# Order of the loads at the start, and the place of the condition gather, in a two-layer kernel with routed experts

## Chip, cores and metric

One core of a Trainium2 chip runs the whole kernel. The metric is device time in microseconds (us) of one execution; the time before is the median of three runs. TensorE is called PE, VectorE DVE, ScalarE ACT, GpSimd POOL and SyncE SP, as in the profile. SP and ACT only issue the plain DMAs here (ACT also computes); POOL issues the indirect ones, whose rows are picked by a list of indices.

## The reference, cut to what matters

The input x has 128 samples of 32 tokens of 256 numbers, 4096 tokens in all, and two index lists with one entry a sample.

```python
# layer 0
H  = x @ W.T                                  # per token
xa = x @ A[idx0].T                            # idx0: one of 8 adapters a sample, rank 16
h  = H + (xa @ Bm[idx0].T) * scalings[idx0]
scores = sigmoid(h @ gate_w.T)                # 8 experts
top, sel = top_k(scores, 2)
routed = sum over k of w2[sel_k] @ (silu(w1[sel_k] @ (h*top_k)) * (w3[sel_k] @ (h*top_k)))
shared = (silu(h @ ws1.T) * (h @ ws3.T)) @ ws2.T
x = x + shared + routed
# layer 1
c = einsum('bct,bcd->bdt', x, weights[idx1])  # a 32x32 mix of the tokens, one of 200 a sample
u = relu(quant(hadamard(c)) @ ternary(w_up).T) ** 2
x = x + quant(hadamard(u)) @ ternary(w_down).T
```

The "adapters' second factors" are Bm (tile bn, and BT in another layout), the "mixes" are `weights[idx1]` (tile wc).

## The kernel before

The 4096 tokens are 32 tiles of 128, in 8 groups of 4 tiles (NG = 8, GT = 4). The work has four stages.

**Loads and set-up (lines 140 to 209).** SP issues the big loads in the order in which they stand in the code, ACT the small ones: GW (gate), i1 (the mixes' indices), i0 (the adapters' indices, repeated on all partitions), sb (scalings). SP's order is wn, AT, xT[0], WT, bn, cst, BT, xT[1] to xT[7], ws, wall in two halves, ud. Each DMA uses one of eight semaphores in turn, so the ninth waits until the first has landed, and so on. cst is one tile of 962 columns with all constants; its first 640 are the identity, the Hadamard matrices and a scaled copy, the rest (from C_TRI on) small tables. Line 162, on POOL, gathers one 32x32 mix a sample (4 KB each, 512 KB) into wc; SP then writes wc to memory (cs, line 168) and reads it back as blocks on a diagonal (bd, four loads, line 181), which POOL has filled with zeros before (line 177). Lines 187 to 197 multiply the gate into W (from wn) and into Bm (from bn), all in one bank pt_gw; two copies on DVE put the result beside WT and BT, so that one matmul yields h and the gate's logits. Lines 203 to 209 make the adapters' mask and two copies of constants on DVE: upper, and idh (the identity in half precision, first used in layer 1).

**Projection and dispatch (lines 211 to 312).** `project(g)` makes pa (x by A, line 214), xa on DVE (line 216, times the mask), then for each of 4 tiles ph = xT by WT (line 226) plus xa by BT (line 229), which ACT copies into hc (line 230). `route(g)` computes scores, ranks and, through the matmuls pp (lines 282 and 283, which count the tokens ahead), the row of each of a token's two copies in an expert-sorted buffer xs in memory: row (285), pick (293), df and dest (298, 299). POOL then issues 8 indirect DMAs (line 303), each of which scatters 128 rows of hc to xs. The loop runs `project(g)` and then `route(g-1)`, so routing is one group behind.

**Slot table, shared expert, experts (lines 314 to 591).** SP reloads x in another layout into the buffers of xT (line 417, x[g] needs project(g) done). route(7), then the slot table (which expert has which of 72 tiles), the padding of xs, and the ternary weights (on DVE, lines 317 to 344). The shared expert runs for groups 0 to 5 (pt_h 429, pgs 439, hids 446, pos 454), then the experts over 36 pairs of tiles: SP fetches xin from xs (line 496) when all scatters have landed, PE transposes and multiplies (504, 530, 547, 556), POOL scatters the results to yt (line 563). Last come the shared expert's groups 6 and 7.

**Layer 1 (lines 594 to 777).** 16 pairs of tiles in a pipeline of 8 steps: combine on POOL (608), the mix by bd (616), Hadamard, quantize, up, relu squared, the outer Hadamard steps on POOL and DVE (694 to 697), quantize, down.

The order of instructions on each engine is made by a scheduler from the program's order and its dependences. The last stage's POOL order is the program's own.

Of the kernel before, what the change touches and what calls it, by code (L numbers as in the profile page):

```python
# [17 lines left out]
B, T = 128, 32  # L18
# [20 lines left out]
C_ID, C_H, C_HS, C_TRI, C_E16, C_N16 = 0, 128, 256, 640, 704, 712  # L39
# [5 lines left out]
def tile_kernel(  # L45
# [20 lines left out]
    nc = tc.nc  # L66
# [14 lines left out]
    def evac(dst, src):  # L81
# [7 lines left out]
    cst = cpool.tile([P, NCONST], F32, name="cst")  # L89
    ident = cst[:, C_ID : C_ID + P]  # L90
# [5 lines left out]
    xT = [  # L96
        cpool.tile([P, 2, GT * P], F32, tag="x", name=f"xT{g}", bufs=NG) for g in range(NG)
    ]
    bd = cpool.tile([P, NT, P], F32, name="bd")
# [4 lines left out]
    idh = cpool.tile([P, P], F16, name="idh")  # L104
# [5 lines left out]
    cs = dram.tile([B, T * T], F32, name="cs")  # L110

    with tc.tile_pool(name="moe", bufs=1) as moe, tc.tile_pool(name="work1", bufs=2) as work1:
# [12 lines left out]
        with tc.tile_pool(name="stage", bufs=1) as stage:  # L125
            wn = stage.tile([P, 2, D], F32, name="wn")
            bn = stage.tile([P, 2, P], F32, name="bn")
            i0 = stage.tile([P, B], I32, name="i0")
            i1 = stage.tile([B, 1], I32, name="i1")
            sb = stage.tile([P, E], F32, name="sb")  # L130
            wc = stage.tile([B, T * T], F32, name="wc")
# [3 lines left out]
            AT = stage.tile([P, 2, P], F32, name="AT")  # L135
# [3 lines left out]

            nc.scalar.dma_start(GW, gate)  # L140
            nc.sync.dma_start(wn, W.rearrange("(c p) d -> p c d", p=P))
            nc.scalar.dma_start(i1, idx1.rearrange("(b o) -> b o", o=1))
            nc.sync.dma_start(AT, AT_)
            nc.sync.dma_start(xT[0], xT_[0])
            nc.scalar.dma_start(
                i0, idx0.rearrange("(o b) -> o b", o=1).partition_broadcast(P)
            )
            nc.scalar.dma_start(
                sb, scal.rearrange("(o e) -> o e", o=1).partition_broadcast(P)
            )  # L150
            nc.sync.dma_start(WT[:, :, :D], WT_)
            nc.sync.dma_start(bn, Bm)
            nc.sync.dma_start(cst, consts)
            nc.sync.dma_start(BT[:, :D], BT_)
            for g in range(1, NG):
                nc.sync.dma_start(xT[g], xT_[g])
            nc.sync.dma_start(ws, shared_)
            nc.sync.dma_start(wall[:, : E * WCOL // 2], experts[:, : E * WCOL // 2])
            nc.sync.dma_start(wall[:, E * WCOL // 2 :], experts[:, E * WCOL // 2 :])
            nc.sync.dma_start(ud, updown)  # L160

            nc.gpsimd.indirect_dma_start(
                out=wc,
                out_offset=None,
                in_=cw.rearrange("s c d -> s (c d)"),
                in_offset=bass.IndirectOffsetOnAxis(ap=i1, axis=0),
            )
            nc.sync.dma_start(cs, wc)

            zeros = stage.tile([P, ROW], F32, name="zeros")  # L170
            cnt = stage.tile([P, E], F32, name="cnt")
# [3 lines left out]
            nc.gpsimd.memset(ones, 1.0)  # L175
            nc.gpsimd.memset(half, HALF)
            nc.gpsimd.memset(bd, 0.0)
            csv = cs.rearrange("(n q) (c d) -> q c n d", q=4, d=T)
            for q in range(4):
                s = slice(32 * q, 32 * q + 32)  # L180
                nc.sync.dma_start(bd[s, :, s], csv[q])


            pt = bank("t", "pt_gw")
# [21 lines left out]
                mask, i0, cst[:, C_N16 : C_N16 + 1], scol, ALU.is_equal, ALU.mult  # L206
            )
            nc.vector.tensor_copy(upper, cst[:, C_U : C_U + P])
            nc.vector.tensor_copy(idh, ident)

            def project(g):
                pa = bank("x", f"pa{g}")
# [181 lines left out]
            def pad():  # L394
# [10 lines left out]
                for e in range(E):  # L405
                    ins = nc.sync.dma_start(xs[bass.ds(rows[e], P), :], zeros).ins
                    tc.declare_no_dep(ins, group="xs", reason="no pair has a row of the padding")
                    tc.add_to_no_dep_group("xs", ins)

            xg = []  # L410
            for g in range(NG):
                project(g)
                if g > 0:
                    route(g - 1)
            for g in range(NG):
                xg.append(cpool.tile([P, GT, D], F32, tag="x", name=f"x{g}", bufs=NG))
                nc.sync.dma_start(xg[g], xt[g])
            route(NG - 1)
            slot_table()
            pad()  # L420
            ternary_weights()
# [50 lines left out]
        with tc.tile_pool(name="work2", bufs=3, reuse_waits="tile") as work:  # L472
# [105 lines left out]
            a, b, c_, tos = {}, {}, {}, {}  # L578
# [281 lines left out]
```

## Time and profile before

| | |
|---|---|
| three timed runs | 452.76, 451.7, 452.3 us; median 452.3 |
| profiled execution | 447.77 us |
| its span, first to last instruction | 446.0 us, mean granted PE clock 0.943 |
| PE / DVE / ACT / POOL busy | 370.8 / 263.1 / 164.4 / 226.5 us |
| projection starts (first ph) | 13.43 us from the span's start |
| first scatter / end of the last | 28.19 / 126.48 us |
| shared expert's first matmul (pgs) | 102.38 us |
| experts' first transpose (pt_s) | 151.59 us |
| layer 1's first combine on POOL | 291.10 us |

How to read it: times in a view run from the span's start. A line of the timeline gives start, length, engine, source line, operation, out<-in with the tiles' names, shape and count, and in brackets how long the engine was idle before and what ended that ("remote" is a semaphore's step that the profile can put down to no instruction; "issue" is a start that no recorded wait explains). The page shows the span also as 40 slices of 11.15 us, each digit a busy share in tenths.

### The profile page before, as it was taken

The numbers are of one execution on the slowest core, as the hardware profiler recorded it, in microseconds if no ns is written. First come the engines' busy times: TensorE is split into PE (matmuls) and PEld (weight loads), VectorE is DVE, ScalarE is ACT, GpSimd is POOL, SyncE is SP. The second block draws the span as 40 slices with busy tenths as digits, with TensorE's granted clock in tenths as the row PEclk, the third lists the DMA queues.
The fourth block names the chain that finished last, engine by engine and source line by source line (L and its number), as shares of the span: only waits on it lengthen the run. The fifth ranks groups of instructions, "written<-read, shape, count | busy, mean of one in ns | idle before, by whom it ended". The sixth has DMA issues, their size and how long they took to land.

```text
span 446.0 us, 6493 instructions
## 1 busy us (share of the span) xinstructions
PE 370.8 (83%) x2055; PEld 289.6 (65%) x2055; DVE 263.1 (59%) x711; ACT 164.4 (37%) x328; POOL 226.5 (51%) x227
## 2 busy tenths in 40 slices
PE   3999292847399899999899899988888878899864
PEld 2676171633166588887787778566777767789753
DVE  0366351527744556555465454345899899988872
ACT  1120110103021144444344243326365664576752
POOL 4037475765820025554655555589656664533340
PEclk9999698797599999999999999999699999999998
DMA  6999343423442134544444412266122220111012
GB/s 225 418 413 294 113 148 134 142 107 128 170 142 61 49 100 152 170 152 139 136 152 146 155 62 75 72 221 208 49 84 104 73 72 25 37 36 49 24 49 71
DMA packets 38881, 57.49 MB, mean 129 GB/s; under 512 B 9277, under 2 KB 28735, under 8 KB 38464
## 3 DMA queue, kind: packets, MB, share of 16 engines
q1 hardware_dynamic: 31600, 39.17, 26.9%
q0 software_dynamic: 6672, 17.84, 10.9%
q8 instruction: 17, 0.28, 0.2%
q10 hardware_dynamic: 576, 0.08, 0.1%
q14 instruction: 16, 0.13, 0.1%
HBM read 33.93 MB, written 24.18 MB: 130 GB/s over the span
## 4 chain that ended last, share of the span: by engine, by line
PE 54%; DVE 21%; POOL 9%; another core or an unknown queue 6%; issue 4%; ACT 4%; DMA 2%; SPq 0%; DVEq 0%; ACTq 0%; POOLq 0%
PE pg L530 15%; PE po L556 7%; PE pgs L439 7%; PE ph L226 5%; POOL x L608 4%; PE ph L229 4%; DVE b L696 4%; PE pr L709 3%; PE pt_s L504 3%; DVE b L697 3%; PE pos L454 3%; POOL a L695 3%; POOL a L694 2%; PE pa L214 2%
## 5 line engine op out<-in xcount | busy, mean ns | idle before, releaser
L563 POOL DMA_INDIRECT yt<-y,to x72 | 70.3, 976 | 89.3 <-DVE cm L513 39.0
L303 POOL DMA_INDIRECT xs<-hc,dest x64 | 65.6, 1024 | 54.7 <-issue 22.2
L530 PE MATMUL pg<-wall,xTs 128*128 x288 | 76.8, 390 | 4.4 <-DVE cm L513 2.2
L530 PEld LDWEIGHTS pg<-wall,xTs 128*128 128x128 f32 x288 | 49.2, 190 | 16.5 <-DVE hid L539 5.5
L539 DVE SCALAR_TENSOR_TENSOR hid<-pg,c,sil 128x128 f32<-128x128 f32 x72 | 25.1, 348 | 47.3 <-ACT sil L538 39.0
L709 PE MATMUL pr<-cst,b 128*128 128x128 f32 x256 | 39.8, 301 | 12.4 <-DVE b L696 10.7
L538 ACT ACTIVATE sil<-pg,c 128x128 f32<-128x128 f32 x72 | 26.5, 368 | 61.8 <-PE pg L530 55.1
L608 POOL TENSOR_TENSOR x<-x,y 128x512 f32<-128x512 f32 x32 | 43.3, 1360 | 6.3 <-PE pgs L439 5.0
L709 PEld LDWEIGHTS pr<-cst,b 128*128 128x128 f32 x256 | 34.5, 207 | 16.1 <-issue 8.1
L230 ACT COPY hc<-ph 128x264 f32<-128x264 f32 x32 | 12.0, 380 | 80.5 <-PE ph L229 34.4
L556 PE MATMUL po<-wall,hidT 128*128 x144 | 37.7, 381 | 0.0
L229 PE MATMUL ph<-BT,xa 128*128 128x264 f32 x64 | 22.4, 438 | 18.4 <-DVE xa L216 18.4
L226 PE MATMUL ph<-WT,xT 128*128 128x264 f32 x128 | 36.3, 411 | 0.3 <-DVE WT L196 0.3
L722 POOL TENSOR_TENSOR dq<-m,kq 128x2 f32<-128x2 f32 x16 | 3.1, 197 | 59.8 <-DVE m L716 59.8
L632 PE MATMUL pf<-cst,yT 128*128 128x256 f32 x128 | 32.4, 391 | 1.4 <-ACT yT L624 1.4
L439 PE MATMUL pgs<-hT,ws 128*128 128x512 f32 x64 | 31.7, 641 | 0.0
L226 PEld LDWEIGHTS ph<-WT,xT 128*128 128x128 f32 x128 | 26.1, 205 | 8.3 <-issue 2.9
L725 ACT ACTIVATE q<-pr,half,sc 128x512 f16<-128x512 f32 x32 | 23.2, 774 | 18.0 <-DVE sc L721 18.0
L696 DVE TENSOR_TENSOR b<-a 128x512 f32<-128x512 f32 x16 | 20.5, 1282 | 13.7 <-POOL a L695 13.7
L229 PEld LDWEIGHTS ph<-BT,xa 128*128 128x128 f32 x64 | 13.0, 213 | 22.7 <-DVE xa L216 19.8
L285 DVE TENSOR_TENSOR row<-pp,cst 128x32 f32<-128x32 f32 x8 | 1.5, 192 | 42.6 <-remote 30.3
L648 ACT ACTIVATE q<-pf,half,sc 128x256 f16<-128x256 f32 x32 | 16.4, 562 | 27.3 <-DVE sc L644 27.2
(132 smaller groups left out, 720.8 us busy)
## 6 DMA issues: line engine op xcount, KB each, us to landing
xin<-xs SPq DMA_DIRECT2D x72, 136.0 KB
y<-yt SPq DMA_DIRECT2D x16, 512.0 KB
xT<-in_xT SPq DMA_DIRECT2D x8, 512.0 KB
x<-in_x SPq DMA_DIRECT2D x8, 512.0 KB
out<-o SPq DMA_DIRECT2D x16, 256.0 KB
wall<-in_experts SPq DMA_DIRECT2D x2, 1536.0 KB
yt<-y,to POOLq DMA_INDIRECT x72
xs<-zeros SPq DMA_DIRECT2D x8, 136.0 KB
```

What stands on the lines that cost most here:

```text
L226: nc.tensor.matmul(ph, xT[g][:, k, cols], WT[:, k], start=(k == 0), stop=False)
L229: nc.tensor.matmul(ph, xa[:, cols], BT, start=False, stop=True)
L303: ins = nc.gpsimd.indirect_dma_start(out=xs, out_offset=bass.IndirectOffsetOnAxis(ap=dest[:, i, n : n + 1], axis=0), in_=hc[g][:, n], in_o ...
L439: nc.tensor.matmul(pg, ws13[:, k, i], hT[:, k], start=(k == 0), stop=(k == 1))
L530: nc.tensor.matmul(pg[:, i].rearrange("p a f -> p (a f)"), xT[:, i, k], wall[:, bass.ds(w + k * D, D)], start=(k == 0), stop=(k == 1),)
L538: nc.scalar.activation(sil[:, i], pg[:, i, 0], AF.Silu, scale=ci)
L556: nc.tensor.matmul(po[:, i], hT[:, i], wall[:, bass.ds(w + 2 * D, D)], start=True, stop=True)
L563: ins = nc.gpsimd.indirect_dma_start(out=yt, out_offset=bass.IndirectOffsetOnAxis(ap=to[:, i : i + 1], axis=0), in_=y[:, i], in_offset=Non ...
L608: nc.gpsimd.tensor_tensor(v, v, y2[:, :, r], ALU.add)
L632: nc.tensor.matmul(pf[:, i], yT[:, k, i * P : (i + 1) * P], had256[k], start=(k == 0), stop=(k == 1),)
L696: nc.vector.tensor_tensor(b[:, 0:2], a[:, 0:2], a[:, 2:4], ALU.add)
L709: nc.tensor.matmul(pr[:, f * P : (f + 1) * P], b[:, f, i * P : (i + 1) * P], had, start=True, stop=True,)
```

## The change

The instructions are the same but for one DMA more (cst is loaded in two parts). They are put in another order:

- SP now issues wn, **bn**, AT, xT[0], WT, **cst's last 322 columns**, BT, xT[1] to xT[4], **cst's first 640 columns**, xT[5] to xT[7], and the rest as before. bn stood behind WT, and cst in one piece behind bn.
- ACT issues GW, i0, sb and then i1; i1 stood second.
- The gather (POOL), cs and the four bd loads (SP) are in a function `mixes()`, called when project(2) and route(1) have been written. On POOL the gather stands, by an order held fixed, between the scatters of group 1 and those of group 2; before, it stood ahead of all scatters. On SP, cs now stands behind x[2], and the bd loads behind x[3]; before, cs stood ahead of x[0] and bd behind x[1].
- idh is copied behind route(7) (its place on DVE is held by the same means, between dest of group 7 and the slot table's st); before, it was copied ahead of the mask.
- On PE, bn's two products stand ahead of pa(0) instead of behind it, and in the first group the adapters' part of tile 0 (line 229) two products earlier. Otherwise PE's order is that of before.

```diff
             nc.scalar.dma_start(GW, gate)
             nc.sync.dma_start(wn, W.rearrange("(c p) d -> p c d", p=P))
-            nc.scalar.dma_start(i1, idx1.rearrange("(b o) -> b o", o=1))
-            nc.sync.dma_start(AT, AT_)
-            nc.sync.dma_start(xT[0], xT_[0])
             nc.scalar.dma_start(
                 i0, idx0.rearrange("(o b) -> o b", o=1).partition_broadcast(P)
             )
+            nc.sync.dma_start(bn, Bm)
             nc.scalar.dma_start(
                 sb, scal.rearrange("(o e) -> o e", o=1).partition_broadcast(P)
             )
+            nc.sync.dma_start(AT, AT_)
+            nc.sync.dma_start(xT[0], xT_[0])
+            nc.scalar.dma_start(i1, idx1.rearrange("(b o) -> b o", o=1))
             nc.sync.dma_start(WT[:, :, :D], WT_)
-            nc.sync.dma_start(bn, Bm)
-            nc.sync.dma_start(cst, consts)
+            nc.sync.dma_start(cst[:, C_TRI:], consts[:, C_TRI:])
             nc.sync.dma_start(BT[:, :D], BT_)
             for g in range(1, NG):
                 nc.sync.dma_start(xT[g], xT_[g])
+                if g == 4:
+                    nc.sync.dma_start(cst[:, :C_TRI], consts[:, :C_TRI])
...
-            nc.gpsimd.indirect_dma_start(
-                out=wc,
-                out_offset=None,
-                in_=cw.rearrange("s c d -> s (c d)"),
-                in_offset=bass.IndirectOffsetOnAxis(ap=i1, axis=0),
-            )
-            nc.sync.dma_start(cs, wc)
...
-            csv = cs.rearrange("(n q) (c d) -> q c n d", q=4, d=T)
-            for q in range(4):
-                s = slice(32 * q, 32 * q + 32)
-                nc.sync.dma_start(bd[s, :, s], csv[q])
...
             nc.vector.tensor_copy(upper, cst[:, C_U : C_U + P])
-            nc.vector.tensor_copy(idh, ident)
...
+            def mixes():
+
+                tc.keep_in_program_order(
+                    nc.gpsimd.indirect_dma_start(
+                        out=wc,
+                        out_offset=None,
+                        in_=cw.rearrange("s c d -> s (c d)"),
+                        in_offset=bass.IndirectOffsetOnAxis(ap=i1, axis=0),
+                    )
+                )
+                nc.sync.dma_start(cs, wc)
+                csv = cs.rearrange("(n q) (c d) -> q c n d", q=4, d=T)
+                for q in range(4):
+                    rows = slice(32 * q, 32 * q + 32)
+                    nc.sync.dma_start(bd[rows, :, rows], csv[q])
+
             xg = []
             for g in range(NG):
                 project(g)
                 if g > 0:
                     route(g - 1)
+                if g == 2:
+                    mixes()
...
             route(NG - 1)
+            tc.keep_in_program_order(nc.vector.tensor_copy(idh, ident))
             slot_table()
```

## The prediction

> **What bounds the kernel now.** I read the page's slices first, then the chain that ended last, then the waits of the stretch in which the chain leaves the program, then GpSimd's (POOL's) timeline there. The slices have PE at 8 or 9 tenths from slice 11 on, but at 7, 3, 9, 9, 8, 9, 9 and lower before, and the window sums say the same: 14.76 us busy of 14.76 between 13.43 and 28.19, but 16.70 of 25.56, 16.15 of 24.49 and 16.84 of 25.19 in the three stretches that follow. All that the change moves acts ahead of 119 us, so that is where it must be priced. The chain of waits, in order of time (start, length, what):
>
> ```profile
> 42.03 5.93 another core or an unknown queue
> ...
> 64.99 11.48 another core or an unknown queue
> ...
> 97.00 3.83 another core or an unknown queue
> 101.28 1.11 PE pt_h L429 x4
> ...
> 118.84 1.22 PE pos L454 x2
> ```
>
> Three times the chain stands in a wait that no instruction ends. After 118.84 it is TensorE, without a hole up to the experts (32.76 us busy of 32.76 up to 151.60). Who waits, between 28 and 104 us (total, times, longest):
>
> ```profile
> DVE row L285 <- remote: 30.3, 3, 11.5
> ACT hc L230 <- remote: 23.9, 6, 6.0
> ...
> PE ph L229 <- DVE xa L216: 18.4, 2, 9.5
> ```
>
> Both "remote" waits are for TensorE's counter alone: the matmuls before them are dispatched long before (the pp of group 2 at 40.77, its reader starts at 50.99). The trace's semaphore records show that counter nearly standing still and then making eight steps between 50.80 and 51.13, again five steps between 76.44 and 76.63, and again from 100.83. POOL's timeline lies beside these times:
>
> ```profile
> 28.19 0.98 POOL L303 DMA_INDIRECT xs<-hc,dest  x1 [22.02 <-DVE s L239]
> ...
> 47.39 0.96 POOL L303 DMA_INDIRECT xs<-hc,dest  x1 [0.30 <-issue]
> 53.75 1.11 POOL L303 DMA_INDIRECT xs<-hc,dest  x1 [5.39 <-issue]
> ...
> 73.17 0.96 POOL L303 DMA_INDIRECT xs<-hc,dest  x1 [0.30 <-issue]
> 78.24 1.02 POOL L303 DMA_INDIRECT xs<-hc,dest  x1 [4.12 <-ACT s L237]
> ...
> 97.55 0.96 POOL L303 DMA_INDIRECT xs<-hc,dest  x1 [0.30 <-issue]
> 103.43 1.13 POOL L303 DMA_INDIRECT xs<-hc,dest  x1 [4.92 <-ACT hT L86]
> ```
>
> The scatters run in bursts of 16, two groups of tokens each, 1.27 us apart (0.96 + 0.30). A burst ends at 48.35, 74.13 and 98.51; its last scatter lands at 49.66 and 75.42 (the third's last packet ends at 99.60); the counter comes free at 50.80, 76.44 and 100.83, so 2.45, 2.31 and 2.32 us after POOL's last issue. Then route needs 2.9, 1.8 and 2.6 us to hand POOL the next rows. The reading that I go by: **a burst of software DMAs holds back TensorE's increments until it has drained.** Why it does so the trace does not say; that the release follows the drain three times within 0.14 us is what I rely on. The period is then 16 scatters plus drain plus route, and the place of PE at 101.28 is set by POOL's first scatter and by what is in the bursts. From 101.28 to 118.84 VectorE (DVE) sets the time (13.84 us busy of 15.41): route(7), the slot table and the ternary weights stand ahead of hids.
>
> **The change part by part.** The profiled execution took 447.77 us, its span is 446.0, with 1.77 around it; the median of the three timed runs is 452.3, 4.5 above. I add differences only, and lay them on the median.
>
> 1. *bn and the small constants ahead of x.* The start now:
>
> ```profile
> 8.76 3.75 PE L214 MATMUL pa<-xT,AT 128*128 128x512 f32 x4 [2.87 <-DMA xT<-in_xT]
> ...
> 12.30 0.86 PE L187 MATMUL pt_gw<-GW,bn 128*128 128x8 f32 x4
> ...
> 13.20 0.17 DVE L196 COPY WT<-pt_gw 128x16 f32<-128x16 f32 x1 [11.78 <-PE pt_gw L187]
> ...
> 13.43 0.94 PE L226 MATMUL ph<-WT,xT 128*128 128x264 f32 x3 [0.27 <-DVE WT L196]
> ...
> 13.64 0.22 DVE L209 CAST idh<-cst 128x128 f16<-128x128 f32 x1
> ```
>
> The reader is to see that bn's matmuls stand behind pa in PE's order and that WT's copy, and with it ph, waits for them. In the new order they follow wn's matmuls (ending 5.89; AT, issued at the place that bn gets, lands at 4.53), in time in which PE is idle. pa ends at 12.51, so ph would start 13.43 - 12.51 = 0.92 sooner. Against it: xT[0] is issued one DMA later on SP (2.24 instead of 1.77), 0.47. I take -0.45, with 0 and -0.92 as ends. The mask and xa are ready well before PE needs them in both orders (xa at 14.84, used at 15.76), and from ph on PE has no hole up to the first scatter, so POOL starts 0.45 sooner, near 27.74.
>
> On the clock: pa's four matmuls take 3.75 here and 1.88 at 18.87, and full clock is recorded from 13.02. The Trainium skill ("TensorE: Matmul & The Clock Gate", Part 1) says that the clock is set by a free-running window of about 3.4 us of activity, not counted from the kernel's start; by it the new hole between bn's matmuls and pa could make the full clock come one window later, which at half speed would turn the gain into an estimated loss of up to 1.2 us. The sum is left at the row.
>
> 2. *i1 last on ACT, cst in two parts, its head behind xT[4].* One more SP issue (0.33 to 0.47 us) in a queue whose next waits are for landed loads. The head (identity, Hadamard) is first read at 93.48 by pt_h. Cost 0; without that cover, a late head would hold PE at pt_h.
>
> 3. *idh moved behind route(7).* At 13.64 it costs nothing (PE is dense); now it stands in DVE's full stretch before hids. Issue to issue it takes 0.14 (13.64 to 13.78), 0.22 at most: +0.14.
>
> 4. *The gather leaves the start.* It is POOL's L162 at 5.05, its data moves from 9.17 to 12.96, and it lands at 13.43, beside the x loads. xT[0] has landed by then (8.17) and later ones are far ahead of use (xT[7] is needed at 86), so removing it gives 0.
>
> 5. *The gather comes between the scatters of groups 1 and 2.* On POOL: 1.13 + 0.30 = 1.43 more in burst 1, behind which group 2's scatters stand. Taken alone this is hidden: POOL is idle for 5.39 us there. But by the reading above burst 1 is now 17 long, and the counter comes free after the gather has drained. Its packets: 8 of 4096 B an engine at 159 ns, 1.27 us, where a scatter has 2 of 4352 B at 190 ns, 0.38: +0.89. So the release moves by 1.43 + 0.89 = +2.32, and with it row, dest, burst 2, burst 3 and PE at 101.28. Ends: 0 (gathers into SBUF do not hold PE) and the gather's own row, issue to landing 13.43 - 5.05 = 8.38, where the same from a scatter is 75.42 - 73.17 = 2.25; that is 1.43 + 6.13 = +7.56. I stay near the low row: at 45 to 51 us the hardware queue moved no packet in the trace, while at 9 to 13 it moved 180 to 410 KB/us beside the gather.
> The Trainium skill ("DMA: Bandwidth & Descriptors", Anatomy of one DMA) gives a software DMA about 2.0 us fixed and the rest at 436 GB/s; by that an estimated 3.2 us for 512 KB, against the 8.38 of the row. By the rule the sum below stays, by the row it would be 5.2 higher.
>
> 6. *SP's queue.* cs now waits for the gather on SP, and x[3], the four bd loads and x[4..7] stand behind it. x[3] waits for PE's project(3) anyway (issued at 50.87 now), the four bd issues take 4.94 us and x[4] is not issued before 59 either; x[g] is first read in shared_down behind 124, bd from the last stage on, behind 281. Cost 0. The bd loads (4 x 1024 packets of 128 B) move from beside burst 1 to beside burst 2; POOL's pitch in burst 1 was 1.27 with them and 1.27 without in burst 2, so 0.
>
> 7. *After 126.* POOL's last scatter ends at 126.48 and PE takes up the experts at 151.59: some 20 us of slack, so POOL's own 1.43 costs nothing there.
>
> Sum: -0.45 + 0.14 + 2.32 = **+2.0 us**: 449.8 for a profiled run, 452.3 + 2.0 = 454.3 as a median.
>
> **The rivals.** (a) *The gather does not hold the counter*: only scatters, which write to memory, do. For it: no gather stands beside a PE at work in this trace. Against: nothing sets its queue apart from theirs. Then -0.45 + 0.14 = -0.3: 452.0, and 451.5 with the whole 0.92. (b) *Faster*: the first hold is not the burst's but that of bd's small packets; they start at 36 us, and PE's counter is first late by more than 2 us at 37.34, 9.1 us into the burst, against 10.3 and 11.8 us in the others. With them gone group 2's rows are there when the gather has been issued, and POOL goes on at 49.3 instead of 53.75: -4.2 - 0.3, so 447.8. It decides if group 2's pp is counted before POOL runs dry at 49.3. Against: bursts 2 and 3 are held as long without any such packet. (c) *Much slower*: the longer burst lets group 2's increments trickle through just before its end; POOL then adds 8 scatters to the same burst, nothing drains until 62, and the pairs become {0,1,2}, {3,4}, {5,6}: PE's release moves from 100.83 to about 112.5, +11.7: 464. (d) That the change does not do what it says: the order of the instructions shows it does; PE's, DVE's and ACT's streams are otherwise the same.
>
> **How the numbers follow.** What a measurement tells from no change is 0.2%, 0.9 us. Forecast 0.50 (its own range 452.9 to 456), (a) 0.22, (b) 0.18, (c) 0.10. Slower: 0.48 of the forecast (a release nearer 1.4 than 2.3 would fall within 0.2%) and (c), 0.58. Faster: (b), and 0.06 of (a) with a better start, 0.24. Within: 0.18. The range reaches down to (b) with room for a second gap, 446.5, and up to the gather's own row, 452.3 - 0.45 + 0.14 + 7.56 = 459.6; it leaves out (c) and the end of (b), under 0.2.
>
> **What would show it.** Right: ph starts near 13.0 and the first scatter near 27.7; the gather follows the 16th scatter; the counter's leap comes near 52.7, group 2's first scatter near 55.6, PE's pt_h near 103.2, all later stretches as long as now. Wrong: group 2's scatter straight behind the gather (b or c), a leap still near 50.4 (a), or a burst 2 or 3 of another length, which would mean that the order of the holds is not tied to the drain.

## The result, and the profile after

The changed kernel took 451.09 us (median of 20 runs, 449.39 to 452.81), the kernel before 451.29 us beside it (20 runs, 446.25 to 452.76). The ratio is 1.0004 with a 95% interval of 0.9983 to 1.0025: no change that can be measured, where +2.0 us was forecast. The profiled executions are 450.77 us after (span 449.0) and 447.77 before (span 446.0); those 3.0 us between two single executions lie within the kernel's own spread, and the one before is among its quicker ones. A run more than 1.5% above the fastest of its kernel on its chip counts as slow and is left out of a ratio: none here, but in set 1 below 10 of 29 runs of the kernel before, 5 of 12 of the loads alone and 8 of 12 of the gather alone.

The start after, TensorE (PE) in its timeline (start, length, engine, line, operation, operands, count; in brackets the idle time ahead of it and what ended it):

```profile
5.66 1.00 PE L177 MATMUL pt_gw<-GW,bn 128*128 128x8 f32 x4
8.39 3.75 PE L203 MATMUL pa<-xT,AT 128*128 128x512 f32 x4 [1.73 <-DMA xT<-in_xT]
11.94 1.68 PE L215 MATMUL ph<-WT,xT 128*128 128x264 f32 x6
```

bn's products now stand ahead of pa, in idle time, and nothing stands between pa and ph: ph starts 3.54 us behind pa's start (4.67 before). pa starts at 8.39 where it was 8.76, although xT[0] is issued at 2.23 instead of 1.77.

GpSimd (POOL) in the same view:

```profile
26.86 1.34 POOL L292 DMA_INDIRECT xs<-hc,dest  x1 [21.98 <-DVE s L228]
...
46.27 0.96 POOL L292 DMA_INDIRECT xs<-hc,dest  x1 [0.30 <-issue]
47.53 0.97 POOL L402 DMA_INDIRECT wc<-in_cond,i  x1 [0.30 <-issue]
53.92 1.12 POOL L292 DMA_INDIRECT xs<-hc,dest  x1 [5.42 <-issue]
```

The first scatter comes 1.33 us sooner (28.19 before), group 2's first 0.17 us later (53.75): the stretch between them grew from 25.56 to 27.06. The later two stretches are 0.28 and 0.37 us longer here (24.77 and 25.56); in the other two executions with a gather in the first burst (set 1 below) they are as before (24.57 and 25.10, 24.54 and 25.18; 24.49 and 25.19 before). PE's pt_h comes at 102.11 (101.28 before, 103.2 forecast) and its first pos at 120.72 (118.84). Of those last 1.88 us, 1.12 arise between row of group 6 and row of group 7 (7.66 for 6.54), where half clock was granted for 10.24 us in one piece and for 6.83 before; that this is the reason is not shown. What waits between 28 and 104 us, then the chain that ended last:

```profile
DVE row L274 <- remote: 33.2, 3, 11.8
ACT hc L219 <- remote: 30.8, 6, 11.4
...
PE ph L218 <- DVE xa L205: 20.7, 2, 10.9
```

```profile
41.01 7.38 another core or an unknown queue
48.80 2.48 another core or an unknown queue
...
65.14 11.78 another core or an unknown queue
...
87.13 11.39 another core or an unknown queue
...
102.11 1.12 PE pt_h L437 x4
```

The same three holes are there. So far the result looks as if 1.3 us of gain and 1.5 us of cost cancelled. The experiments show the cost on one kind of chip only.

### The profile page after: what moved, and what is told of

It reads as the page before. It is cut to its first block, busy times and chain, and to the rows that moved or that the text cites. A ratio compares the mean times of both kernels' runs of the same rounds, so it can differ in the third digit from the quotient of the medians.

```text
span 449.0 us, 6497 instructions
## 1 busy us (share of the span) xinstructions
PE 369.9 (82%) x2055; PEld 288.2 (64%) x2055; DVE 263.0 (59%) x711; ACT 164.4 (37%) x328; POOL 226.1 (50%) x227
## 4 chain that ended last, share of the span: by engine, by line
PE 48%; DVE 21%; POOL 9%; another core or an unknown queue 9%; issue 5%; ACT 3%; DMA 3%; SPq 1%; DVEq 0%; POOLq 0%; ACTq 0%
PE pg L538 13%; PE pgs L447 7%; PE po L564 6%; PE ph L215 5%; DVE b L704 4%; DVE b L705 3%; PE pr L717 3%; POOL x L616 3%; PE ph L218 3%; PE pos L462 3%; POOL a L703 3%; PE pt_s L512 3%; POOL a L702 3%; PE pa L203 2%
## 5 line engine op out<-in xcount | busy, mean ns | idle before, releaser
L538 PE MATMUL pg<-wall,xTs 128*128 x288 | 78.2, 396 | 7.0 <-DVE hid L547 3.6
L717 PE MATMUL pr<-cst,b 128*128 128x128 f32 x256 | 37.9, 291 | 13.7 <-DVE b L704 11.3
L717 PEld LDWEIGHTS pr<-cst,b 128*128 128x128 f32 x256 | 32.7, 197 | 17.5 <-issue 8.1
L447 PE MATMUL pgs<-hT,ws 128*128 128x512 f32 x64 | 33.0, 663 | 0.0
L733 ACT ACTIVATE q<-pr,half,sc 128x512 f16<-128x512 f32 x32 | 23.2, 774 | 16.9 <-DVE sc L729 16.9
L704 DVE TENSOR_TENSOR b<-a 128x512 f32<-128x512 f32 x16 | 20.5, 1282 | 13.7 <-POOL a L703 13.7
```

The costliest lines, as they stand in the source:

```text
L447: nc.tensor.matmul(pg, ws13[:, k, i], hT[:, k], start=(k == 0), stop=(k == 1))
L538: nc.tensor.matmul(pg[:, i].rearrange("p a f -> p (a f)"), xT[:, i, k], wall[:, bass.ds(w + k * D, D)], start=(k == 0), stop=(k == 1),)
L704: nc.vector.tensor_tensor(b[:, 0:2], a[:, 0:2], a[:, 2:4], ALU.add)
L717: nc.tensor.matmul(pr[:, f * P : (f + 1) * P], b[:, f, i * P : (i + 1) * P], had, start=True, stop=True,)
```

## The experiments

**Theory**: the loads' order gains between one and two microseconds at the start, and the gather costs about as much in the first burst, because software DMAs in a burst hold back the increments of TensorE's semaphore. **Rivals**: the gather holds nothing (rival a of the prediction); the start's gain is no gain of the loads but a matter of when the full clock is granted; or the hold is not a property of the burst.

Five sets were run, on five chips; the first of them behaves as the chip of the result does, and may be the same. Each set's ratios are against the kernel before on the same chip. Marks are of single profiled executions, in us: the *first stretch* runs from the first scatter to group 2's first, *row* is the start of that DVE instruction for a group, *PE's restart* the start of the first pos, behind the last hole, and the *scatters' end* the end of POOL's last scatter to xs.

### Set 1: the parts of the change, and a second gather

*The loads alone* (gather, cs and bd at the start as before; idh late):

```diff
             nc.sync.dma_start(ud, updown)
+            nc.gpsimd.indirect_dma_start(
...
+            nc.sync.dma_start(cs, wc)
...
-                if g == 2:
-                    mixes()
```

> The loads in the new order and the late copy of idh, with the gather, its store and the reloads where they stood before. Theory T (a burst of software DMAs holds TensorE's counter until it has drained): the earlier start passes through every burst, first scatter near 26.9 us as in the changed kernel, row of group 2 near 49.7 (50.99 before, 51.33 changed), row of group 6 near 99.8, and the time 1.2 us below before, ratio 0.997. Rival R (the first hold ends by something that stands fixed against the loads): row of group 2 stays near 51 and the ratio is 1.000.

Measured: 0.9961 (0.9915 to 1.0007); over all runs the median is 449.33, of the kernel before 448.66. Marks: first scatter 27.93, first stretch 25.61, row of group 2 at 50.79 and of group 6 at 100.86, all three marks with an expectation 1.0 to 1.1 us later than expected.

*The gather alone*, an edit of the kernel before (its loads and idh stay; the gather, cs and bd leave the start):

```diff
                     route(g - 1)
+                if g == 2:
+                    mixes()
```

> The loads and idh in the old order, only the gather, its store and the reloads amid the dispatch. Theory T: first scatter 28.2, the counter's release 1.7 us later because the burst is one DMA longer, row of group 2 near 52.7, row of group 6 near 102.7, time +1.7 us, ratio 1.004. Rival R: the gather costs nothing, row of group 2 near 51, ratio 1.000.

Measured: 0.9948 (0.9888 to 1.0009), a ratio that rests on 4 of the 12 runs; over all of them the median is 450.87, 2.2 above the kernel before, so the total says neither loss nor gain. Marks: first scatter 29.70, first stretch 26.58, so +1.0 by the mark; row of group 2 is 24.24 us behind the first scatter (22.80 in the kernel before).

*The whole change, with the gather behind all scatters*:

```diff
-                if g == 2:
-                    mixes()
...
             route(NG - 1)
+            mixes()
```

> The changed kernel with the gather behind the scatters of all groups. Theory T: no burst holds the gather, row of group 2 near 49.7, row of group 6 near 99.8, time 1.2 us below before, ratio 0.997. Rival: SP now issues the store and the reloads ahead of the experts' rows; if these come later than TensorE's end of the shared groups (151.6 before) the time is above before.

Measured: 1.0004 (0.9973 to 1.0035), median 448.17. Marks: first scatter 27.43, first stretch 25.52, row of group 2 at 50.38 and of group 6 at 100.16.

*The gather twice* (the second into a tile of its own; the output is the same):

```diff
                 tc.keep_in_program_order(
                     nc.gpsimd.indirect_dma_start(
                         out=wc,
...
+                tc.keep_in_program_order(
+                    nc.gpsimd.indirect_dma_start(
+                        out=wc2,
...
+                nc.sync.dma_start(cs2, wc2)
```

> The changed kernel with the gather done twice in the same place, into two tiles, and stored twice. Theory T: the first burst has 18 DMAs, so the release moves by the same 1.7 us again: row of group 2 near 53.0 (51.33 changed), later bursts unchanged in length, row of group 6 near 103.3. Rival R: row of group 2 stays at 51.3.

Measured: 448.01 us in one run; first scatter 26.91, first stretch 27.29. POOL's timeline in it:

```profile
47.50 0.97 POOL L404 DMA_INDIRECT wc<-in_cond,i  x1 [0.30 <-issue]
48.77 0.95 POOL L412 DMA_INDIRECT wc<-in_cond,i  x1 [0.30 <-issue]
54.20 1.10 POOL L294 DMA_INDIRECT xs<-hc,dest  x1 [4.47 <-issue]
```

The second gather adds 0.23 us to the stretch, where the prediction's sum (1.27 of issue and 0.89 of drain) has 2.16. Counted from the first scatter, TensorE's counter leaps 22.61 us later in the kernel before (50.80) and 24.34 us later with one gather (51.20). But in the kernel before the leap is 1.36 us behind the burst's last packet (49.44), and with the gather it is 0.04 us ahead of it (51.24). In the gather alone the counter comes free in parts, from 22.78 us behind the first scatter (52.48) to 24.22 (53.92), all ahead of the last packet (54.14). With two gathers it comes free in two parts: the first 22.79 us behind the first scatter (49.70, with both gathers in flight and 2.5 us behind the last scatter's end), the rest at 25.67 (52.58; the last packet ends at 53.64). In none of the three does the release wait for the whole burst to drain, as it seemed to do in the kernel before.

Both expectations for two gathers were missed: row of group 2 came at 49.79, ahead of 51.3 and 53.0. Its scatter was late all the same, because on DVE dest (53.21) stands behind xa, and xa waited for the second part until 52.60:

```profile
49.79 0.19 DVE L276 TENSOR_TENSOR row<-pp,cst 128x32 f32<-128x32 f32 x1 [9.89 <-remote]
...
52.60 0.69 DVE L207 TENSOR_TENSOR xa<-pa,mask 128x512 f32<-128x512 f32 x1 [1.69 <-remote]
53.21 0.16 DVE L290 CAST dest<-df 128x8 int32<-128x8 f32 x1
```

The marks of this set agree: 25.52 to 25.61 without the gather in the burst, 26.58 to 27.29 with it. Its totals settle nothing: the runs of the kernel before went from 444.73 to 452.92, the ratios don't add up (the two halves below 1, the one without the gather's cost at 1.0004), and the medians over all runs put the three in another order.

### Set 2: both kernels once more, four gathers, the second scatters last

> The changed kernel once more, unaltered, to see how far its marks move between executions. Theory (the start gains some 1.3 us, the gather in the first burst costs some 1.5 us, later bursts carry the sum on and the rest of the program is as before): the first scatter within 0.5 us of 26.9, group 2's first scatter 27.1 +- 0.5 behind it, and a median within 0.25% of the kernel before. Rival (the profiled execution shown was an unlucky one, and the gather really costs nothing): the distance from the first scatter to group 2's first is 25.6 as in the kernel before, and the kernel is 1 us faster.

> The kernel before once more, unaltered. Theory: first scatter within 0.5 us of 28.2, group 2's first scatter 25.6 +- 0.3 behind it, PE back on the shared experts (pos) near 118.8. Rival (the start is a matter of where the clock's window falls and not of the order of the loads): the first scatter moves by a us or more between two executions of the same kernel, into the range of the changed one (26.9).

Measured: the changed kernel 411.66 us, the kernel before 414.07 (23 runs; 412.55 in its profile), ratio **0.9951 (0.9924 to 0.9977)**. Nothing in the kernels differs from the first pair, and they are 39 and 37 us shorter. Both expectations were missed: the first scatter came at 27.69 and 27.62, and group 2's first 21.89 and 20.53 us behind it. The waits between 28 and 104 us of the kernel before on this chip (total, times, longest):

```profile
ACT hc L230 <- PE ph L229: 25.6, 18, 2.8
POOL xs L303 <- DVE s L239: 21.4, 1, 21.4
...
DVE row L285 <- PE pp L283: 8.2, 5, 1.8
```

No wait is "remote" any more, and the longest wait of row is 1.8 us instead of 11.5. POOL's timeline in it, at the place where the first burst ended before:

```profile
46.88 0.96 POOL L303 DMA_INDIRECT xs<-hc,dest  x1 [0.30 <-DMA xs<-hc,dest]
48.15 0.96 POOL L303 DMA_INDIRECT xs<-hc,dest  x1 [0.30 <-ACT hc L230]
49.41 0.96 POOL L303 DMA_INDIRECT xs<-hc,dest  x1 [0.30 <-issue]
```

The 64 scatters are one burst without a gap, from 27.62 to 111.54, and TensorE goes on beside it all the time. Both executions run the same instructions in the same order, so each instruction that waits for an engine (a reader of it) can be laid beside itself. How much later a reader starts than the end of what it waits for and of the instruction before it on its own engine, at most, from the first scatter to the last (POOL's own left out):

| kernel before | readers of TensorE | of VectorE | of ScalarE | PE's restart (pos) | span |
|---|---|---|---|---|---|
| first pair | 9.74 us late | 0.05 | 0.05 | 118.84 | 446.0 |
| this chip | 0.11 | 0.06 | 0.05 | 86.25 | 410.8 |

Two things follow. In the first pair it is TensorE's counter alone that is held, as the prediction had it. The records of VectorE's and ScalarE's increments have gaps there too, but their readers are in time: ScalarE's s ends at 60.39 and has its next record at 77.38, and the DVE instruction that reads it starts at 60.42. So a gap in the records is not yet a late increment, and where the expectations of sets 3 and 4 speak of the increments of all engines, that is more than was seen. And an unbroken burst of 64 scatters does not hold TensorE's on this chip. The slices of PE (busy share in tenths, 40 equal slices of the span) show it at a glance, first the changed kernel in the first pair, then on a chip of this kind (set 4):

```profile
PE   4997292837399899999999979999688887899864
```

```profile
PE   4999999469979999999999999887888888899863
```

What the gather does here stands in POOL's timeline of the changed kernel:

```profile
47.03 0.96 POOL L292 DMA_INDIRECT xs<-hc,dest  x1 [0.30 <-DMA xs<-hc,dest]
48.30 0.97 POOL L402 DMA_INDIRECT wc<-in_cond,i  x1 [0.30 <-issue]
49.57 0.99 POOL L292 DMA_INDIRECT xs<-hc,dest  x1 [0.31 <-DMA xs<-hc,dest]
```

It takes 1.27 us of POOL (48.30 to 49.57), the scatters end 1.45 us later (112.99 for 111.54), and PE's restart doesn't move (86.41 for 86.25).

*Four gathers* (three more, each into a tile of its own, as the second above):

> The changed kernel with three more gathers of the same rows behind the first, into tiles of their own (the output is unchanged). The prediction's reading (every software DMA of the burst holds TensorE's counter, and the release comes when the last has drained): each gather adds 1.27 us of issue and 0.89 of drain, so group 2's first scatter comes 27.1 + 6.5 = 33.6 us behind the first scatter. Rival (only the scatters, which write to memory, hold the counter; a gather costs POOL's issue time alone): the counter leaps 2.5 us behind the 16th scatter's end, near 49.7, group 2's rows are there at 53, and its first scatter follows the fourth gather at once or within 1 us, some 26 to 27 us behind the first. A value between says that the counter comes free in parts.

Measured: 413.14 us in one run; first stretch 26.07, scatters' end 116.48, PE's restart 86.01. Here the slack behind the scatters is used up. PE at its first turn to the experts:

```profile
120.19 0.99 PE L545 MATMUL pt_s<-cst,xin 128*128 128x128 f32 x4 [0.47 <-DMA xin<-xs]
...
122.23 0.44 PE L545 MATMUL pt_s<-cst,xin 128*128 128x128 f32 x2 [0.45 <-DMA xin<-xs]
```

PE waits for the fetches of the rows, which stand behind the scatters. The first expert's product is 0.72 us later than in the changed kernel of the same chip; then the clock halves from 125.1 to 128.6, and by the tenth product it is 2.02.

*The second choices' scatters behind the last group's* (in the program's text 36 scatters in one go at the end):

```diff
-                for n in range(GT):
-                    for i in range(2):
+                scatter(g, 0)
...
             route(NG - 1)
+            for g in range(NG):
+                scatter(g, 1)
```

> The changed kernel with the scatters in another order: behind each group's routing only the four scatters of the first choices; the 32 scatters of the second choices all behind the last group's routing (the output is unchanged). Theory (a long burst of software DMAs holds back TensorE's increments until it drains): bursts of 4 take 5.1 us, less than the 7.4 us that TensorE needs for a group, so POOL drains between groups and the waits for the remote counter vanish; a group's period falls from 12.5 us to about 8, the last group's rows are routed near 90 us instead of 110; then 36 scatters in one go, 46 us, hold TensorE's counter, and the shared experts stall until about 136, so the time grows by some 10 to 15 us, to 460 to 466. Rival (the counter is held by something else, for instance by the loads of x or by the number of groups in flight): the holds stay near 25 us for two groups, and the time moves by what POOL's last scatter moves alone.

Measured: 410.97 us, 0.9927 (0.9901 to 0.9953). The marks are those of the changed kernel (PE's restart 86.79, scatters' end 113.39), and the edit did not make the short bursts it was meant to make. POOL issues from the first scatter to the last without a pause, and 37 scatters have started when the last group's rows are known (dest of group 7, 76.50), of which only 28 can be first choices: the scheduler has put second choices into the pauses. The two repeats below have the same 37. So these three runs compare two orders of one unbroken burst, and could not have told the theory from the rival on any chip.

### Sets 3 and 4: the same questions on other chips, and bn put back

The gather two groups later, and bn's load where it stood:

```diff
-                if g == 2:
+                if g == 4:
                     mixes()
```

```diff
-            nc.sync.dma_start(bn, Bm)
...
             nc.sync.dma_start(WT[:, :, :D], WT_)
+            nc.sync.dma_start(bn, Bm)
```

> The kernel with the second choices' scatters all behind the last group, once more. In the last set, on a chip on which no engine's increments came late, it had no hold to take away. If this chip holds increments as the first one did (kernel before at about 450 us): theory (the increments of all engines come late while GpSimd issues software DMAs without a pause) gives a first half without holds, the last group's row near 75 to 90 us instead of 109, then a hold until some 2.5 us behind the last scatter, at 115 to 135 us, and a total between -10 us (if PE gets through the shared experts with increments that trickle) and +15 us. Rival (the holds come with the amount of traffic and not with GpSimd's bursts): the holds are where they were, two groups long. If the chip doesn't hold (kernel before at about 413 us): 411 +- 1, as in the last set.

> The changed kernel with three more gathers behind the first, once more. On a chip that holds increments: by the prediction's reading (the release follows the drain of the whole burst) group 2's first scatter comes 27.1 + 3 x 2.16 = 33.6 us behind the first scatter; by the rival (a gather costs GpSimd's issue time alone, and the counter comes free 2.5 us behind the last scatter) it comes 26 to 27 us behind. On a chip that doesn't hold: 26.1 us as in the last set (16 scatters and 4 gathers of 1.3 us), and PE's restart unchanged.

> The changed kernel with the gather and the four loads behind it two groups later (behind group 3's scatters instead of group 1's). On a chip that holds: the first stretch (first scatter to group 2's first) falls back from 27.1 to 25.6 us and the second grows from 24.8 to 26.3, if the gather's price is that of a DMA more in the burst wherever it stands; rival (the price belonged to the first burst alone, which also has the loads of x beside it): both are near 25. On a chip that doesn't hold: 20.5 in the first stretch and 21.9 in the second, and no change at PE.

> The changed kernel with one load put back: the adapters' second factors (bn) behind WT on the queue, where they stood; all else as changed. Theory (the gain of the start is bn's: its matmuls and the copy of their result no longer stand between pa and ph): ph starts 0.8 to 1.0 us later than in the changed kernel, near 12.9 to 13.4, with the distance from pa's start to ph's start back at 4.2 to 4.7 us (4.67 before, 3.55 changed). Rival (the gain is that of x or the constants): the distance stays near 3.55.

Set 3's chip didn't hold increments either (kernel before 413.53). The second scatters last: 410.82 us, 0.9934 (0.9909 to 0.996). Four gathers: 413.55 us, first stretch 25.66, PE's restart 85.51. The gather two groups later: 411.68 us, stretches of 20.63 and 21.70, PE's restart 86.03. bn put back behind WT: 413.03 us, and its start is

```profile
7.92 3.75 PE L203 MATMUL pa<-xT,AT 128*128 128x512 f32 x4 [2.13 <-DMA xT<-in_xT]
11.46 0.86 PE L177 MATMUL pt_gw<-GW,bn 128*128 128x8 f32 x4
12.59 3.01 PE L215 MATMUL ph<-WT,xT 128*128 128x264 f32 x6 [0.27 <-DVE WT L186]
```

The distance from pa to ph is back at 4.67, as the theory had it. But more is seen: six products of ph take 3.01 us, where they take 1.68 in the changed kernel above. Full clock was granted at 16.17 here and at 12.29 there, and the first scatter comes at 29.19, 2.3 us later.

> The second choices' scatters all behind the last group. If this chip holds increments (kernel before near 450 us): theory (increments of all engines come late while GpSimd issues software DMAs without a pause) gives a first half almost without holds, the last group's row near 75 to 90 us instead of 109, then one long hold until some 2.5 us behind the last scatter, and a total between -10 and +15 us of the kernel before. Rival (holds come with traffic, not with bursts): the holds stay where they were. If it doesn't hold: 0.993 of the kernel before, as on the two chips that didn't.

> Three more gathers behind the first. On a chip that holds: by the prediction's reading (release when the whole burst has drained) group 2's first scatter comes 33.6 us behind the first scatter; by the rival (a gather costs issue time alone, the counter comes free 2.5 us behind the last scatter) 26 to 27 us. On a chip that doesn't hold: 25.7 to 26.1, as on the two others.

> The gather two groups later. On a chip that holds: stretches of 25.6 and 26.3 us (first scatter to group 2's, group 2's to group 4's) if its price is that of one more DMA in a burst, wherever; both near 25 if the price belongs to the first burst alone. On a chip that doesn't hold: 20.6 and 21.7, as measured on the last one.

> The changed kernel unaltered. On a chip that holds: 1.000 +- 0.003 of the kernel before, its first scatter 27.0 +- 0.5 and group 2's 27.1 +- 0.5 behind it. On a chip that doesn't: 0.995 +- 0.003, the gather's 1.35 us on GpSimd seen in its scatters' end (113.0) but not in PE's restart (86.3).

Set 4's chip didn't hold either (kernel before 413.22). The changed kernel: 411.39 us, **0.9955 (0.9932 to 0.9977)**, first scatter 26.79, scatters' end 112.10, PE's restart 85.52. The second scatters last: 411.18, 0.9957 (0.9933 to 0.998). Four gathers: 414.09. The gather later: 411.03, stretches of 20.64 and 21.71. So the questions that need a chip that holds (four gathers, the gather's place) have no answer, as none of the later chips held increments, and short bursts were made on none.

### Set 5: the two halves side by side

> The loads' new order alone (the gather and the loads behind it stay at the start), once more. On a chip that doesn't hold increments: theory (PE's stream from ph on sets PE's restart there, and bn's matmuls out of its way start ph about 1 us sooner) 0.996 +- 0.003 of the kernel before, ph 3.55 us behind pa, PE's restart at 85.5 to 86.4 as in the whole change. Rival (the gain comes from the gather's leaving the start): 1.000 +- 0.002. On a chip that holds: 0.996 to 1.000.

> The gather and its loads amid the dispatch alone (loads in the old order), once more. On a chip that doesn't hold: theory (GpSimd's 1.35 us more lies off the path, the scatters end 1.35 us later and PE's restart doesn't move) 1.000 +- 0.003 of the kernel before, ph 4.7 us behind pa. Rival (the gather at the start cost something beside the loads): 0.996. On a chip that holds: the burst's stretch 26.6 us where it is 25.6 before, and 0.995 to 1.004.

Measured, on a chip that didn't hold (kernel before 413.94): the loads alone 412.31 us, **0.9962 (0.9938 to 0.9985)**; the gather alone 413.37 us, **0.9997 (0.9973 to 1.0022)**. PE's restart in the loads alone is at 85.75, as expected. In the gather alone it is at 88.81, but there the first scatter is late too (30.12, full clock at 17.53): from the one to the other it takes 58.69 us, and 58.63 in the kernel before in set 2. The start of the gather alone, which has the loads in the old order:

```profile
8.43 3.75 PE L202 MATMUL pa<-xT,AT 128*128 128x512 f32 x4 [2.43 <-DMA xT<-in_xT]
11.97 0.86 PE L175 MATMUL pt_gw<-GW,bn 128*128 128x8 f32 x4
13.10 4.66 PE L214 MATMUL ph<-WT,xT 128*128 128x264 f32 x10 [0.27 <-DVE WT L184]
```

On this kind of chip the gain is the loads', and moving the gather costs nothing that can be measured (the two intervals overlap; PE's restart in set 2 says the same).

### The start, over all executions

Ahead of the first scatter no reader of TensorE starts late even where they do later (0.07 us at most), so all twenty profiled executions can be laid together: fifteen with bn's load ahead of pa, five with it behind. Of the five, four have the whole old order of the loads; bn put back in set 3 is the one that differs in bn alone.

| | pa starts | ph starts | full clock granted | first scatter |
|---|---|---|---|---|
| bn ahead (15) | 8.52 | 12.01 | 12.87 (11.25 to 14.41) | 27.20 (26.25 to 28.03) |
| bn behind (5) | 8.43 | 13.02 | 15.08 (11.99 to 17.53) | 28.97 (27.62 to 30.12) |

The means differ by 1.77 us at the first scatter. 1.01 of it is there at ph; the other 0.76 is clock: in each of the twenty, the way from ph to the first scatter is 14.7 us plus half of what ph has to wait for the full clock, within 0.2 us (a wait of 0 where full clock came first; ph at 13.10 and full clock at 17.53 give 16.9, measured 17.02; 11.94 and 12.29 give 14.9, measured 14.93).

## Why the prediction was wrong, step by step

It named the changed places rightly and failed in two terms of its sum, the start (1) and the gather (5), and in the reading that carried the second. A slip at its head changed no term: the slices at 7, 3, 9, 9, 8, 9, 9 are the 10th to the 16th, so PE is dense from slice 12 on, not 11.

1. *bn ahead of x* failed in size: -0.45 was taken, with ends of 0 and -0.92; at the first scatter it is -1.33 in the pair of the result and -1.77 in the mean of the twenty, of which -1.01 is there at ph. The term against it, +0.47 for xT[0]'s later issue, was not there: pa's start is 8.52 against 8.43 in the mean, 0.09 later, and earlier in the pair of the result. Which transfer set its landing was not shown. And the clock went the other way than feared: with bn's products ahead, full clock came by 14.41 at the latest in fifteen executions; with them behind it came at 16.17, 16.70 and 17.53 in three of five. That the products ahead of pa are what brings it sooner is argued from this, not shown; five is few. The Trainium skill ("TensorE: Matmul & The Clock Gate", Part 1) describes the gate as a window of about 3.4 us that runs freely and is not started by the kernel. The traces agree: half-clock stretches last 3.4, 6.8, 10.2 or 13.7 us, and the moment of full clock moves by up to 3.2 us between executions of the fifteen. The estimate made from the page, a loss of up to 1.2 us, has the wrong sign here: it weighed the new hole between bn's products and pa, and not that the same work begins sooner; that this is the reason is argued too.
2. *i1 and cst*: 0 was right as far as a trace shows it; no wait for either.
3. *idh*: +0.14 was right. In the first pair the way from row of group 7 to PE's restart (pos less row) grew from 11.28 to 11.42. On the chips without holds pos less row is 11.52 both times (86.25 - 74.73, 86.41 - 74.89), so there it is not seen.
4. *The gather leaves the start*: 0 was right (the gather's half alone 0.9997). One reading behind it was off: the landing at 8.17 is i0's; xT[0] lands at 8.62, still ahead of the gather's first packet at 9.17.
5. *The gather in the first burst* is **the step that failed in its mechanism**. Predicted +2.32; measured +1.50 in the first stretch of the changed kernel, +1.02 in the gather alone, with 0.23 for a second gather. The release itself came 1.73 us later by one gather (24.34 less 22.61 from the first scatter). Of that, 1.27 is the gather's issue (1.43 in the sum), 0.25 is drain behind POOL's last issue (2.70 for 2.45; 0.89 in the sum), and 0.21 the sixteen scatters themselves (20.37 for 20.16). With two gathers its first part came only 0.18 later. Counted to row of group 6 the gather costs +1.95 in the changed kernel and +1.11 alone (74.78 and 73.94 behind the first scatter, 72.83 before), so the size is known to about 1 us. Under it lies the larger error, the sentence that "a burst of software DMAs holds back TensorE's increments until it has drained". Three holds that ended 2.31 to 2.45 us behind POOL's last issue were taken for a law of the burst. With a gather in the burst the release doesn't follow the drain, and on four chips a burst four times as long holds nothing. There the gather costs POOL 1.3 us that no one waits for, and +2.32 becomes 0.
6. *SP's queue* and the bd loads: 0 was right on both kinds. Rival (b), that bd's small packets cause the first hold, fell with it: in the changed kernel they are gone from the first burst, and its hold is as long.
7. *Behind 126*: the slack of 20 us belonged to a held kernel. Without holds PE turns to the experts at 119 to 120, the changed kernel's scatters end at 112 to 113, and four gathers instead of one already make PE wait. For the one gather of the change, 0 was right all the same.

Put together: on chips without holds, -1.8 at the start and nothing for the gather gives 0.9957 on 414; measured were 0.9951 and 0.9955, on the two of the four where the whole change ran. Where increments are held, -1.8 + 1.0 to 1.5 + 0.14 gives about -0.7 to -0.2 us; measured was 1.0004 with 1 us to either side. This sum is made afterwards from marks, and the one profiled pair doesn't follow it behind group 2 (PE's restart is 1.88 later). Rival (a), 452.0 or 451.5 us, was nearest to the result, but by luck: with the gather in the burst row of group 2 did come 1.4 to 1.7 us later from the first scatter (24.24 and 24.47 for 22.80), and a gain at the start that was larger than foreseen made up for it.

What stays open: why increments are late in the first pair and in set 1 and not on the four other chips; a property of the chip, of the core's place on it, or of what else runs there would all look the same here. Set 1's totals spread too far to confirm or deny its marks, and no second chip of that kind came to settle it. Whether shorter bursts would help on such a chip was not tried. The kernel with the second scatters last beats the kernel before on three chips without holds (0.9927, 0.9934, 0.9957), but not the changed kernel by more than the intervals hold.

## What to carry to other kernels

A pattern that repeats three times in one trace is still one chip: before a wait that the profile cannot name ("remote") is priced as a law, run the same kernel on a second chip. Read in the trace whether an edit made the order it was written for; a scheduler may have filled the pauses that it was to leave. Price work on TensorE's first microseconds with its clock: there, each microsecond by which the full clock comes later costs half a microsecond, and small products put into the idle time ahead of the first large one cost nothing and may bring it sooner. Slack that lies behind a stall is lent by the stall; work hidden in it comes to light where the stall is absent.

## What the runs showed of the hardware

One kernel took about 450 us in the first pair and in set 1, and about 414 on four other chips, and the difference lies almost whole in one stage: PE's restart at 118.84 against 86.25, 32.6 us of 35.2 between two profiles. In the first of them (kernel before, first pair) what waits for TensorE starts up to 9.74 us late in that stage, and 0.11 in set 2's; what waits for VectorE and ScalarE is in time in both.

Where TensorE's increments come late, they do so only while POOL scatters. Four executions of the first pair and set 1 can be laid beside an execution of the same instructions in the same order on a free chip (both kernels, the loads alone, the gather alone). In them the readers of TensorE start up to 8.5 to 10.0 us late while POOL scatters to xs and up to 1.9 to 3.4 while it scatters to yt; ahead of the first scatter, between the two runs of scatters (129.0 to 163.1 in the kernel before) and behind the last it is 0.16 at most, as on the free chips. The amount of traffic alone does not do it: in the kernel before 422 GB/s move between 13.43 and 28.19, with no reader late, and 254, 134 and 127 in the three stretches with holds. Nor did its gather at the start, alone in its queue (packets from 9.17 to 12.80): the step of PE's counter behind pa follows pa's end at 12.51 by 0.01. The prediction's "no gather stands beside a PE at work" overlooked that. Why TensorE's increments come late beside POOL's scatters on one chip and not on another is open.

The page itself tells the two kinds apart, in its list of DMA issues (operands, queue, count, size, time to landing), first the first pair's, then set 2's, both of the kernel before:

```profile
xin<-xs SPq DMA_DIRECT2D x72, 136.0 KB
```

```profile
xin<-xs SPq DMA_DIRECT2D x72, 136.0 KB, 2.4
```

In the first trace increments are missing from the records (97 on one of the queue's semaphores for 17 DMAs, 272 in the second), so the profile can't say when such a load landed and leaves the time out.

The totals also move with the clock's windows. In the changed kernel the half clock fell on two windows of 3.4 us in the middle of the program (at 261.5 and 319.5) in the first pair, and on one (at 278.3) in set 4; the kernel before had 6.8 at 278.2 and 3.4 at 397.7 in set 2. One window of 3.4 us at half clock, at a place where PE has no hole, is by that half some 1.7 us of work: as much as the loads of this change gain.
